# Softmax division moved behind the value product, cross attention by pairs of tiles, last residuals on ScalarE and GpSimd

## The chip, the core and the metric

The kernel runs on one core of a Trainium2 chip. The core has TensorE (PE; its weight loads are shown apart, as PEld), VectorE (DVE), ScalarE (ACT), GpSimd (POOL) and SyncE (SP, which issues most transfers). Each works through its own instruction queue in order; semaphores order them against each other. The metric is the device time of one execution in microseconds, here the median of three runs.

## What is computed

One decoder block on 2 x 1024 tokens of width 256, all in float32: self attention with 16 heads and a relative bias, cross attention onto 77 context tokens with 16 heads of width 16, and a mixture of 8 experts, two chosen per token. Each part is a residual on a normalised input. Cut to what the change touches:

```python
x = x + self_attention(layernorm(x))       # ends in its own layernorm with gamma_a, beta_a

q, k, v = heads(layernorm(x) @ Wq), heads(ctx @ Wk), heads(ctx @ Wv)   # q, k divided by DK ** 0.25
scores = where(mask == 0, -1e9, q @ k.T)   # (2, 16, 1024, 77)
attn = softmax(scores)                     # over the 77 context tokens
x = x + concat_heads(attn @ v) @ Wu + bu

h = layernorm(x)
x = x + layernorm(0.5 * gelu(h @ shared_W + shared_b)
                  + sum of the two best experts of softmax(h @ gate_W)) * gamma + beta
```

## The kernel before

**Layout.** `xs` holds all tokens in SBUF as 16 tiles of 128 tokens; four tiles are a chunk `c` (0 to 3). All PSUM tiles up to the experts come from one ring of eight banks (`one`, line 83), reused in program order.

**Stages.** A loop over `n` runs the two streams of self attention (`stream_a`, `stream_b`, `times_v`), with small jobs put between them by the tables `between`, `settle` and `ask`. There are 16 halves `h` of attention, four for each chunk; `collect(h)` divides by the sums and writes a chunk's output to a tile `o`, which is normalised and added to `xs`. For chunks 0 and 1 `settle` does this in the streams, with ScalarE and GpSimd. For chunks 2 and 3 (`h` 14 and 15) it is done behind the streams by VectorE, in `o_gamma` (line 1083) and `o_add` (line 1089): eight instructions per chunk.

**Order.** Behind the loop the order is written out by hand as a list of words (line 1124 on). The program issues them one after the other, so the list fixes each engine's own queue. `exps_b` and `times_v` are the end of the streams; at `close` the streams' buffers are given up and SyncE loads weights for the experts' routing; `weights` starts the first expert's load.

**Cross attention**, for each tile `i`: `scores` (TensorE, four banks), `masked` (VectorE adds the mask and takes the row maxima), `less` (GpSimd subtracts them), `exps` (ScalarE), `sums` (VectorE sums 77 columns per head and takes the reciprocal), `shares` (GpSimd multiplies all 16 x 77 exponentials by it), `turn` (TensorE transposes 16 heads, ScalarE copies them into `PT`). For each chunk: `attend(c, G)` (the values times `PT`, 512 columns, copied to `oT` by ScalarE) and `output(c, u)` (times `Wu`, added to `xs` by VectorE). `query` and `q_*` prepare a chunk's queries; `add_bu` adds the bias.

**Routing.** When a chunk has its output, `stats`, `dev`, `off`, `norm` normalise it and store it to `xnd`, `flip` transposes it, `gate` computes the logits, `choose`, `rank`, `place`, `hots` and `invert` find the expert slots of its tokens, and after the last chunk `owners` and `pick` give the rows that the experts gather. `shared` (the shared layer) is put between. Chunks 0 and 1 form one group of routing, chunks 2 and 3 one each. The experts' loop follows; its gathers go to `xgs`.

**Normalisation.** `norm_scale` (line 134) adds the epsilon on VectorE and raises to the power -0.5 on GpSimd. `offsets` (line 167) makes the offset on VectorE, and `scale` (line 178) applies both on ScalarE.

## Time and profile before

| what | value |
|---|---|
| three runs | 976.96, 978.7 and 988.31 us, median 978.7 |
| profiled execution | 986.99 us; span from first to last instruction 985.3 us |
| mean granted TensorE clock | 0.965 of full |
| PE busy | 922.7 us (94% of the span) |
| DVE busy | 579.4 us (59%) |
| ACT busy | 544.1 us (55%) |
| POOL busy | 403.5 us (41%) |
| last `times_v` ends | about 501.8 us |
| `pick` starts | 666.9 us |

The profile is one execution, and its times are microseconds from its first instruction. Line numbers (L700) are those of the kernel before. In a row of groups, `out<-in` names the tiles, `x12` the count, then come the busy time of all and the mean ns of one, then the engine's idle time just ahead of them and what ended it. A granted clock of 1.00 is full speed. TensorE's matmuls in float32 are recorded twice each, transposes once.

### The profile page before, as it was taken

The numbers are of one execution on the slowest core, as the hardware profiler recorded it, in microseconds if no ns is written. First come the engines' busy times: TensorE is split into PE (matmuls) and PEld (weight loads), VectorE is DVE, ScalarE is ACT, GpSimd is POOL, SyncE is SP. The second block draws the span as 40 slices with busy tenths as digits, with TensorE's granted clock in tenths as the row PEclk, the third lists the DMA queues.
The fourth block names the chain that finished last, engine by engine and source line by source line (L and its number), as shares of the span: only waits on it lengthen the run. The fifth ranks groups of instructions, "written<-read, shape, count | busy, mean of one in ns | idle before, by whom it ended". The sixth has DMA issues, their size and how long they took to land.

```text
span 985.3 us, 16174 instructions
## 1 busy us (share of the span) xinstructions
PE 922.7 (94%) x6080; PEld 542.9 (55%) x6080; DVE 579.4 (59%) x1172; ACT 544.1 (55%) x1079; POOL 403.5 (41%) x344
## 2 busy tenths in 40 slices
PE   9999999999999999999947999998999999999983
...
DVE  5874668878888797987589998471111031011117
...
PEclk9999999999999999999976999689999999999997
...
GB/s 172 59 1 2 2 2 1 2 1 1 2 1 2 1 2 1 1 1 1 1 0 18 1 23 22 27 17 264 307 196 156 206 180 153 206 308 329 132 145 125
DMA packets 65162, 75.62 MB, mean 77 GB/s; under 512 B 17967, under 2 KB 57036, under 8 KB 65076
## 3 DMA queue, kind: packets, MB, share of 16 engines
...
## 4 chain that ended last, share of the span: by engine, by line
PE 72%; DVE 15%; DMA 9%; issue 2%; ACT 1%; POOL 1%; SPq 0%; DVEq 0%; POOLq 0%; ACTq 0%
PE sA L549 14%; PE av L612 13%; PE sB L595 11%; PE po L1515 9%; PE ph L1496 9%; DMA pairs<-y,to_row 7%; PE pp L502 3%; PE pb L394 2%; PE pv L340 1%; DVE cm L700 1%; DVE cs L712 1%; PE pq L664 1%; DVE scrap L696 1%; PE idle L252 1%; DVE xs L1094 1%
## 5 line engine op out<-in xcount | busy, mean ns | idle before, releaser
L556 DVE TENSOR_REDUCE mx<-sA 128x1 f32<-128x512 f32 x512 | 317.4, 683 | 95.4 <-PE sB L595 88.4
L603 ACT ACTIVATE pt<-sB 128x512 f32<-128x512 f32 x512 | 264.8, 603 | 63.1 <-PE sB L595 63.0
L549 PE MATMUL sA<-kT,scrap 32*128 32x512 f32 x1024 | 253.8, 619 | 0.0
L595 PE MATMUL sB<-qB,kT 32*128 32x512 f32 x1024 | 247.6, 616 | 0.0
L625 POOL TENSOR_TENSOR avs<-avs,part 128x512 f32<-128x512 f32 x112 | 142.1, 1269 | 231.0 <-ACT part L624 225.7
L1503 ACT ACTIVATE hT<-ph,b1s 128x256 f32<-128x256 f32 (+1 forms) x184 | 77.7, 424 | 184.6 <-PE ph L1496 179.7
L549 PEld LDWEIGHTS sA<-kT,scrap 32*128 32x128 f32 x1024 | 100.4, 183 | 82.3 <-ACT pt L603 54.5
L612 PE MATMUL av<-pt,vaug 128*32 128x512 f32 x1024 | 137.4, 605 | 3.2 <-DVE mx L556 3.2
L595 PEld LDWEIGHTS sB<-qB,kT 32*128 32x128 f32 x1024 | 97.7, 183 | 37.9 <-issue 30.1
L1522 DVE TENSOR_TENSOR y<-po,b 128x512 f32<-128x512 f32 (+1 forms) x23 | 13.0, 564 | 176.4 <-PE po L1515 169.7
L1496 PE MATMUL ph<-xgT,w 128*128 128x256 f32 (+1 forms) x576 | 109.3, 334 | 1.3 <-DMA w<-in_L_ffn_W_dram 0.7
L1515 PE MATMUL po<-w,hT 128*128 128x256 f32 x432 | 105.2, 382 | 3.4 <-DVE y L1522 3.3
L1496 PEld LDWEIGHTS ph<-xgT,w 128*128 128x128 f32 x576 | 91.3, 191 | 21.4 <-ACT hT L1503 7.5
L1515 PEld LDWEIGHTS po<-w,hT 128*128 128x128 f32 x432 | 77.7, 190 | 14.4 <-DVE y L1522 5.5
L1526 POOL DMA_INDIRECT pairs<-y,to_row x35 | 35.3, 1007 | 115.1 <-DMA pairs<-y,to_row 79.4
L1466 POOL DMA_INDIRECT xg<-xnd,from_row x35 | 34.3, 979 | 104.5 <-PE px L1482 64.2
L612 PEld LDWEIGHTS av<-pt,vaug 128*32 128x32 f32 x1024 | 21.0, 109 | 100.4 <-DVE mx L556 91.4
L624 ACT COPY part<-av 128x512 f32<-128x512 f32 x108 | 65.7, 609 | 5.4 <-PE av L612 5.1
L138 POOL TENSOR_TENSOR rstd<-rstd,nhalf 128x4 f32<-128x4 f32 x20 | 21.7, 1084 | 71.2 <-DVE rstd L137 70.8
L729 ACT COPY PT<-ppT 77x512 f32<-77x512 f32 x64 | 32.7, 588 | 2.2 <-PE ppT L728 1.5
L1515 PE MATMUL po<-xnT,hT 128*128 128x256 f32 x128 | 31.8, 383 | 1.9 <-DVE y L1522 1.9
L194 PE MATMUL pxT<-ident,xn 128*128 128x128 f32 x96 | 17.5, 305 | 16.7 <-ACT xn L184 16.6
...
## 6 DMA issues: line engine op xcount, KB each, us to landing
...
```

What stands on the lines that cost most here:

```text
L549: nc.tensor.matmul(s, lhsT=units[h // 4, "q"][r0 : r0 + 32, q0 : q0 + P], rhs=units[h // 4, "k", g % 2][r0 : r0 + 32, 512 * kh : 512 * kh ...
L556: nc.vector.tensor_reduce(largest[h][:, qt, hh : hh + 1, kh], s, AX.X, ALU.max)
L595: nc.tensor.matmul(s, lhsT=units[h // 4, "k", g % 2][r0 : r0 + 32, kt * P : (kt + 1) * P], rhs=shifted[h][r0 : r0 + 32, :], start=True, st ...
L603: nc.scalar.activation(powers[m, hh], s, AF.Exp, scale=1.0 / 16.0)
L612: nc.tensor.matmul(av[32 * hh : 32 * hh + 32, :], lhsT=vaug[:, kt, 4 * g + hh, :, b], rhs=powers.pop((m, hh)), start=True, stop=True,)
L624: copy(part, av)
L625: nc.gpsimd.tensor_tensor(sums[h], sums[h], part, ALU.add)
L1466: fetched[i] = nc.gpsimd.indirect_dma_start(out=xg[:, s, :], out_offset=None, in_=xnd[:, :], in_offset=bass.IndirectOffsetOnAxis(ap=from_r ...
L1496: nc.tensor.matmul(ph[:, hc % group, :], lhsT=w1[:, kc, hc * P : (hc + 1) * P], rhs=xgT[:, kc, :], start=(kc == 0), stop=(kc == 1),)
L1503: hidden[i] = nc.scalar.activation(hT[:, hc, :], ph[:, hc % group, :], AF.Gelu, bias=b1s[:, i, hc : hc + 1])
L1515: nc.tensor.matmul(po[:, s, :], lhsT=hT[:, hc, s * P : (s + 1) * P], rhs=w2[:, hc, :], start=(hc == 0), stop=(hc == NH - 1),)
L1526: nc.gpsimd.indirect_dma_start(out=pairs[:, :], out_offset=bass.IndirectOffsetOnAxis(ap=to_row[:, k : k + 1], axis=0), in_=y[:, s, :], in_ ...
```

## The change

The exponentials are transposed as they are. A new `fold` on GpSimd adds columns 38 to 75 of a head to columns 0 to 37 and copies column 76, so VectorE sums 39 columns instead of 77; ScalarE spreads the 16 reciprocals over 256 columns (`wide`). `shares` is gone. A new `divisors(k)` transposes the spread reciprocals of two tiles and copies them to `oT`; `attend(k)`, now for a pair of tiles, multiplies them by the product with the values on VectorE. `output(k)` is also by pairs. For chunks 2 and 3 of self attention the residual is done as in `settle`: `o_off` and `o_norm` with ScalarE, `o_gamma` and `o_add` by halves on GpSimd. The epsilon and the offsets move to GpSimd everywhere. The `o` tiles move to a pool that stays open, and the experts' gather buffers `xgs` are laid into them. There are 27 idle matmuls at the start instead of 30, and the list of words is a new one.

```diff
@@ -122,6 +122,7 @@
     xnT = const.tile([P, 2, N], F32, name="xnT")
+    kept = ctx.enter_context(tc.tile_pool(name="kept", bufs=1))
     keep = ExitStack()
@@ -134,7 +135,7 @@
         r = small.tile([P, 4], F32, tag="rstd", name="rstd")
-        nc.vector.tensor_scalar(r[:, :n], mv[:, :, 1], eps, None, ALU.add)
+        nc.gpsimd.tensor_scalar(r[:, :n], mv[:, :, 1], eps, None, ALU.add)
         nc.gpsimd.tensor_tensor(r[:, :n], r[:, :n], nhalf[:, :n], ALU.pow)
@@ -168,9 +169,10 @@
         if live is not None:
-            nc.vector.tensor_tensor(r[:, :4], r[:, :4], live, ALU.mult)
+            nc.gpsimd.tensor_tensor(r[:, :4], r[:, :4], live, ALU.mult)
         off = small.tile([P, 4], F32, tag="off", name=f"off{c}")
-        nc.vector.scalar_tensor_tensor(off, mv[:, :, 0], -1.0, r[:, :4], ALU.mult, ALU.mult)
+        nc.gpsimd.tensor_tensor(off, mv[:, :, 0], r[:, :4], ALU.mult)
+        nc.gpsimd.tensor_scalar(off, off, -1.0, None, ALU.mult)
         if dst is None:
@@ -248,7 +250,7 @@
     idle = one("idle")
-    for _ in range(30):
+    for _ in range(27):
         nc.tensor.matmul(idle[:, :P], lhsT=ident, rhs=ident, start=True, stop=True)
@@ -627,7 +629,7 @@
         if (b, qb) not in outs:
-            outs[b, qb] = kp.tile([P, 4, D], F32, tag="o", name=f"o{b}{qb}", bufs=2)
+            outs[b, qb] = kept.tile([P, 4, D], F32, tag="o", name=f"o{b}{qb}", bufs=2)
         o, avs = outs[b, qb], sums.pop(h)
@@ -687,7 +689,7 @@
-    maxima = {}
+    maxima, halved, one_over = {}, {}, {}
@@ -707,57 +709,78 @@
+    def fold(i):
+        st, half = sts[i % 4], T2 // 2
+        halved[i] = cr2.tile([P, H, half + 1], F32, tag="halved", name=f"halved{i}")
+        nc.gpsimd.tensor_tensor(
+            halved[i][:, :, :half], st[:, :, :half], st[:, :, half : 2 * half], ALU.add
+        )
+        nc.gpsimd.tensor_copy(halved[i][:, :, half:], st[:, :, 2 * half :])
     def sums_of(i):
-        maxima[i] = small.tile([P, H], F32, tag="cs", name="cs")
-        nc.vector.tensor_reduce(maxima[i], sts[i % 4], AX.X, ALU.add)
-        nc.vector.reciprocal(maxima[i], maxima[i])
-    def shares(i):
-        st, cs = sts[i % 4], maxima.pop(i)
-        nc.gpsimd.tensor_tensor(st, st, cs.unsqueeze(2).to_broadcast([P, H, T2]), ALU.mult)
+        cs = small.tile([P, H], F32, tag="cs", name="cs")
+        rc = small.tile([P, H], F32, tag="rc", name="rc")
+        nc.vector.tensor_reduce(cs, halved.pop(i), AX.X, ALU.add)
+        nc.vector.reciprocal(rc, cs)
+        one_over[i] = cr2.tile([P, H, DH], F32, tag="wide", name=f"wide{i}", bufs=4)
+        nc.scalar.copy(one_over[i], rc.unsqueeze(2).to_broadcast([P, H, DH]))
     def turn(i):
-        c, t = i // 4, i % 4
-        if c not in PTs:
-            PTs[c] = cr2.tile([P, H, 512], F32, tag="PT", name=f"PT{c}")
+        k, t = i // 2, i % 2
+        if k not in PTs:
+            PTs[k] = cr2.tile([P, H, 2 * P], F32, tag="PT", name=f"PT{k}")
         st = sts[i % 4]
-        for k in range(4):
+        for q in range(4):
             pp = one("ppT").rearrange("p (h f) -> p h f", f=P)
             for h in range(4):
-                nc.tensor.transpose(pp[:T2, h, :], st[:, 4 * k + h, :], ident)
-            nc.scalar.copy(PTs[c][:T2, 4 * k : 4 * k + 4, P * t : P * t + P], pp[:T2, :, :])
-    def attend(c, G):
-        b, PT = c // 2, PTs[c]
-        if c not in oTs:
-            oTs[c] = cr2.tile([P, 2, 512], F32, tag="oT", name=f"oT{c}")
-        po = one("pco")
-        for i in range(2):
-            for r in range(4):
-                h = 8 * G + 2 * r + i
-                nc.tensor.matmul(
-                    po[32 * r : 32 * r + 32, :],
-                    lhsT=vx[:T2, b, h, :, :].rearrange("p i d -> p (i d)"),
-                    rhs=PT[:T2, h, :],
-                    start=(i == 0),
-                    stop=(i == 1),
+                nc.tensor.transpose(pp[:T2, h, :], st[:, 4 * q + h, :], ident)
+            nc.scalar.copy(PTs[k][:T2, 4 * q : 4 * q + 4, P * t : P * t + P], pp[:T2, :, :])
+    def divisors(k):
+        oTs[k] = cr2.tile([P, 2, 2 * P], F32, tag="oT", name=f"oT{k}")
+        pr = one("pr").rearrange("p (g f) -> p g f", g=2)
+        for t in range(2):
+            rc = one_over.pop(2 * k + t).rearrange("p h d -> p (h d)")
+            for G in range(2):
+                nc.tensor.transpose(
+                    pr[:, G, P * t : P * t + P], rc[:, P * G : P * G + P], ident
                 )
-        nc.scalar.copy(oTs[c][:, G, :], po)
-    def output(c, u):
+        nc.scalar.copy(oTs[k], pr)
+    def attend(k):
+        b, PT = k // 4, PTs.pop(k)
+        po = one("pco").rearrange("p (g f) -> p g f", g=2)
+        for G in range(2):
+            for i in range(2):
+                for r in range(4):
+                    h = 8 * G + 2 * r + i
+                    nc.tensor.matmul(
+                        po[32 * r : 32 * r + 32, G, :],
+                        lhsT=vx[:T2, b, h, :, :].rearrange("p i d -> p (i d)"),
+                        rhs=PT[:T2, h, :],
+                        start=(i == 0),
+                        stop=(i == 1),
+                    )
+        nc.vector.tensor_tensor(oTs[k], oTs[k], po, ALU.mult)
+    def output(k):
         pu = one("pu").rearrange("p (t f) -> p t f", f=D)
+        oT = oTs.pop(k)
         for t in range(2):
 ...
                     pu[:, t, :],
-                    lhsT=oTs[c][:, G, P * (2 * u + t) : P * (2 * u + t) + P],
+                    lhsT=oT[:, G, P * t : P * t + P],
                     rhs=cwu[:, G, :],
 ...
                 )
-        x2 = xs[:, 4 * c + 2 * u : 4 * c + 2 * u + 2, :]
+        x2 = xs[:, 2 * k : 2 * k + 2, :]
         nc.vector.tensor_tensor(x2, x2, pu, ALU.add)
@@ -1078,20 +1101,23 @@
-    def o_gamma(h):
+    def o_off(h):
         c, o = out_of(h)
-        mv = moments.pop(("o", c))[1]
-        for t in range(4):
-            nc.vector.scalar_tensor_tensor(
-                o[:, t, :], o[:, t, :], mv[:, t, 0:1], gamma_a, ALU.subtract, ALU.mult
-            )
-    def o_add(h):
+        offsets(("o", c), None, o)
+    def o_norm(h):
         c, o = out_of(h)
-        r = tokens.pop(("o", c))
-        for t in range(4):
-            x1 = xs[:, 4 * c + t, :]
-            nc.vector.scalar_tensor_tensor(x1, o[:, t, :], r[:, t : t + 1], x1, ALU.mult, ALU.add)
+        scale(("o", c), range(4), o)
+    def o_gamma(h, u):
+        o2 = out_of(h)[1][:, 2 * u : 2 * u + 2, :]
+        g2 = gamma_a.unsqueeze(1).to_broadcast([P, 2, D])
+        nc.gpsimd.tensor_tensor(o2, o2, g2, ALU.mult)
+    def o_add(h, u):
+        c, o = out_of(h)
+        x2 = xs[:, 4 * c + 2 * u : 4 * c + 2 * u + 2, :]
+        nc.gpsimd.tensor_tensor(x2, x2, o[:, 2 * u : 2 * u + 2, :], ALU.add)
@@ -1105,6 +1131,8 @@
         o_dev=o_dev,
+        o_off=o_off,
+        o_norm=o_norm,
         o_gamma=o_gamma,
@@ -1112,7 +1140,8 @@
         sums=sums_of,
-        shares=shares,
+        fold=fold,
+        divisors=divisors,
         q_stats=measure,
@@ -1123,36 +1152,38 @@
         exps_b:119 times_v:118:1 exps_b:120 times_v:119:1 exps_b:121 times_v:120:1
-        exps_b:122 times_v:121:1 collect:14 exps_b:123 times_v:122:1 o_stats:14
-        exps_b:124 times_v:123:0 scores:0 o_dev:14 exps_b:125 masked:0 times_v:124:0
-        exps_b:126 times_v:125:0 exps_b:127 times_v:126:0 o_gamma:14 scores:1 masked:1
-        less:1 scores:2 masked:2 o_add:14 times_v:127:0 less:0 collect:15 exps:1
-        q_stats:2 q_dev:2 o_stats:15 exps:0 o_dev:15 sums:0 o_gamma:15 q_off:2 less:2
-        sums:1 exps:2 o_add:15 sums:2 shares:0 q_norm:2 q_stats:3 close shares:1
-        q_flip:2:1 add_bu:2 shares:2 scores:3 masked:3 q_flip:2:0 turn:0 less:3 scores:4
-        q_dev:3 exps:3 masked:4 turn:1 sums:3 less:4 shares:3 scores:5 exps:4 masked:5
-        turn:2 sums:4 query:2:1 query:2:0 less:5 shares:4 constant:0 scores:6 exps:5
-        masked:6 turn:3 sums:5 less:6 shares:5 constant:1 scores:7 exps:6 attend:0:0
-        masked:7 attend:0:1 turn:4 sums:6 q_off:3 less:7 shares:6 constant:2 scores:8
-        q_norm:3 exps:7 masked:8 output:0:1 stats:0:1 output:0:0 q_flip:3:1 add_bu:3
-        turn:5 sums:7 less:8 shares:7 constant:3 scores:9 q_flip:3:0 exps:8 masked:9
-        turn:6 sums:8 less:9 shares:8 constant:4 scores:10 query:3:0 exps:9 masked:10
-        query:3:1 turn:7 sums:9 less:10 shares:9 constant:5 scores:11 stats:0:0 exps:10
-        attend:1:0 masked:11 dev:0 attend:1:1 turn:8 sums:10 off:0 less:11 norm:0
-        shares:10 constant:6 scores:12 exps:11 masked:12 output:1:1 stats:1:1 output:1:0
-        turn:9 sums:11 less:12 shares:11 constant:7 scores:13 exps:12 masked:13
-        flip:0:1:0 flip:0:0:0 turn:10 sums:12 gate:0 less:13 shares:12 constant:8
-        scores:14 exps:13 masked:14 turn:11 sums:13 less:14 shares:13 constant:9
-        scores:15 stats:1:0 exps:14 attend:2:0 masked:15 dev:1 attend:2:1 turn:12
-        sums:14 off:1 less:15 norm:1 shares:14 exps:15 output:2:1 output:2:0 turn:13
-        sums:15 shares:15 stats:2:1 flip:1:1:0 stats:2:0 flip:1:0:0 turn:14 dev:2 gate:1
-        choose:0 earlier:1 turn:15 attend:3:0 attend:3:1 off:2 rank:0 place:0 output:3:0
-        stats:3:0 output:3:1 norm:2 stats:3:1 dev:3 flip:2:1:0 flip:2:0:0 shared:0:0
-        hots:0:0 off:3 hots:1:0 norm:3 gate:2 hots:0:1 flip:3:1:1 choose:1 flip:3:0:0
-        shared:1:1 gate:3 shared:3:0 rank:1 earlier:2 invert:0 choose:2 place:1 hots:2:0
-        rank:2 hots:2:1 totals shared:3:1 hots:1:1 invert:1 place:2 hots:3:0 shared:0:1
-        hots:3:1 filled:0 invert:3 owners invert:2 shared:2:0 filled:1 weights filled:2
-        filled:3 pick shared:2:1 rows biases shared:1:0
+        exps_b:122 times_v:121:1 collect:14 exps_b:123 times_v:122:1 exps_b:124
+        times_v:123:0 scores:0 masked:0 exps_b:125 times_v:124:1 exps_b:126
+        times_v:125:0 o_stats:14 exps_b:127 times_v:126:1 scores:1 o_dev:14
+        times_v:127:0 masked:1 scores:2 less:1 collect:15 o_off:14 exps:1 o_stats:15
+        less:0 o_norm:14 o_dev:15 o_gamma:14:0 exps:0 o_off:15 close o_add:14:0
+        o_gamma:14:1 o_add:14:1 o_norm:15 masked:2 q_stats:2 fold:0 o_gamma:15:1
+        o_gamma:15:0 fold:1 less:2 q_dev:2 q_off:2 sums:0 turn:0 o_add:15:0 turn:1
+        sums:1 o_add:15:1 scores:3 masked:3 exps:2 fold:2 divisors:0 attend:0 turn:2
+        less:3 q_stats:3 q_norm:2 scores:4 exps:3 q_flip:2:1 add_bu:2 masked:4 sums:2
+        q_flip:2:0 output:0 stats:0:0 turn:3 fold:3 sums:3 less:4 query:2:0 scores:5
+        exps:4 q_dev:3 masked:5 divisors:1 attend:1 turn:4 fold:4 sums:4 less:5 q_off:3
+        scores:6 exps:5 q_norm:3 masked:6 output:1 stats:0:1 turn:5 fold:5 sums:5 less:6
+        dev:0 scores:7 exps:6 query:2:1 masked:7 off:0 divisors:2 norm:0 attend:2 turn:6
+        fold:6 sums:6 less:7 scores:8 exps:7 q_flip:3:1 add_bu:3 q_flip:3:0 constant:0
+        masked:8 output:2 stats:1:0 turn:7 fold:7 sums:7 constant:1 less:8 flip:0:1:1
+        flip:0:0:1 scores:9 exps:8 constant:2 masked:9 divisors:3 gate:0 constant:3
+        attend:3 turn:8 fold:8 sums:8 less:9 constant:4 scores:10 exps:9 query:3:1
+        constant:5 masked:10 output:3 stats:1:1 turn:9 fold:9 sums:9 constant:6 less:10
+        query:3:0 dev:1 scores:11 exps:10 constant:7 masked:11 off:1 divisors:4
+        constant:8 norm:1 attend:4 turn:10 fold:10 sums:10 less:11 constant:9 scores:12
+        exps:11 masked:12 output:4 stats:2:0 turn:11 fold:11 sums:11 less:12 flip:1:1:1
+        flip:1:0:0 scores:13 exps:12 masked:13 divisors:5 gate:1 choose:0 attend:5
+        turn:12 fold:12 sums:12 less:13 scores:14 exps:13 rank:0 masked:14 output:5
+        stats:2:1 turn:13 fold:13 sums:13 place:0 less:14 dev:2 hots:1:1 off:2 scores:15
+        exps:14 divisors:6 norm:2 masked:15 attend:6 turn:14 flip:2:1:0 hots:0:1 fold:14
+        flip:2:0:0 sums:14 earlier:1 less:15 output:6 gate:2 exps:15 shared:1:0 turn:15
+        choose:1 hots:0:0 rank:1 fold:15 sums:15 divisors:7 place:1 stats:3:0 attend:7
+        earlier:2 output:7 stats:3:1 invert:0 shared:2:1 dev:3 hots:2:1 off:3 norm:3
+        shared:0:1 filled:0 flip:3:1:0 flip:3:0:0 hots:2:0 hots:1:0 gate:3 invert:1
+        choose:2 invert:2 rank:2 filled:1 shared:2:0 filled:2 totals shared:1:1
+        shared:0:0 place:2 hots:3:1 hots:3:0 invert:3 owners filled:3 pick weights rows
+        shared:3:0 biases shared:3:1
     """.split()
@@ -1448,7 +1479,7 @@
         ff2 = later.enter_context(tc.tile_pool(name="ff2", bufs=1))
-        xgs = [ff2.tile([P, 2, D], F32, name=f"xg_{k}") for k in range(3)]
+        xgs = [outs[1, k // 2][:, 2 * (k % 2) : 2 * (k % 2) + 2, :] for k in range(3)]
         xgTs = [ff2.tile([P, 2, 2 * P], F32, name=f"xgT_{k}") for k in range(2)]
```

## The prediction

> **What bounds the kernel now.** I read the page's slices first, to find where TensorE is not busy at full clock: only slices 20 to 27, some 490 to 690 us.
>
> ```profile
> PE   9999999999999999999947999998999999999983
> DVE  5874668878888797987589998471111031011117
> PEclk9999999999999999999976999689999999999997
> ```
>
> Before it the two attention streams hold TensorE, after it the experts do; the change leaves both nearly alone. So I asked for the busy time of each engine in stretches of 10 us (PE, PEld, DVE, ACT, POOL, granted clock, DMA share, GB/s):
>
> ```profile
> 500.00:510.00 10.00, 2.68 (x16) 0.95 (x14) 9.86 (x15) 3.05 (x3) 7.43 (x5) 0.79 0.00 0
> 510.00:520.00 10.00, 0.00 (x0) 0.00 (x0) 9.66 (x21) 1.23 (x1) 7.07 (x5) 0.50 0.00 0
> ...
> 550.00:560.00 10.00, 10.00 (x70) 6.32 (x62) 9.86 (x15) 5.69 (x10) 8.72 (x8) 1.00 0.00 0
> ...
> 590.00:600.00 10.00, 10.00 (x87) 6.82 (x89) 9.79 (x19) 5.91 (x11) 9.44 (x7) 1.00 0.00 0
> ...
> 620.00:630.00 10.00, 10.00 (x42) 6.41 (x33) 1.41 (x7) 3.14 (x6) 0.00 (x0) 0.50 0.16 54
> ```
>
> Three stages: an opening (500 to 540), VectorE full and TensorE empty or at half clock; a middle (540 to 612), both full; a tail (612 to 667, where `pick` starts), TensorE busy but at half clock from 614 to 632. The chain of work that ended last gives the opening to VectorE's residuals and the tail to TensorE:
>
> ```profile
> 505.00 4.01 DVE xs L1094 x4
> ...
> 515.92 5.14 DVE o L1085 x4
> ...
> 522.97 5.59 DVE xs L1094 x4
> ...
> 616.44 6.98 PE pco L739 x32
> ...
> 626.94 6.21 PE pu L753 x16
> ```
>
> In the middle the chain names VectorE, but the windows show TensorE equally full: freeing VectorE there gives nothing. The prices, from the groups by shape, 480 to 690 us:
>
> ```profile
> L718 POOL TENSOR_TENSOR scrap<-scrap,cs 128x1232 f32<-128x1232 f32 x12 | 27.3, 2272 | 5.4 <-DVE cs L713 5.4
> L705 POOL TENSOR_TENSOR scrap<-scrap,cm 128x1232 f32<-128x1232 f32 x12 | 27.2, 2266 | 3.1 <-DVE cm L700 2.5 <-PE pu L753 0.6
> L712 DVE TENSOR_REDUCE cs<-scrap 128x16 f32<-128x1232 f32 x12 | 17.1, 1427 | 0.0
> L1085 DVE SCALAR_TENSOR_TENSOR o<-o,bnmv('o', 3)_5809,gamma_a 128x256 f32<-128x256 f32 x4 | 5.2, 1364 | 0.0
> L1085 DVE SCALAR_TENSOR_TENSOR o<-o,bnmv('o', 2)_5617,gamma_a 128x256 f32<-128x256 f32 x4 | 2.7, 747 | 0.0
> ```
>
> **Streams, before 490 us.** `offsets` goes from one VectorE instruction (0.15 us) to two or three on GpSimd, and the epsilon add too. GpSimd's tiny casts cost 0.19 us, so 0.4 to 0.6 us a call; it is 59% idle. Only the queue matters: at chunks 0 and 1, `scale` on ScalarE follows `offsets` at once, and the GpSimd queue then holds an accumulation (308.20 to 309.47) ahead of it. ScalarE's scale, at 308.04 now, waits till about 310, with the next exponentials behind it: 0 if they catch up, 2 us each if not; I take 1 us, twice, +2. Three idle matmuls fewer: 60 records took 9.86 us, six are 0.7 to 1.0 us, and the first transposes (11.1 us) stand right behind them with their first tile ready at about 9.4: -0.7. Sum +1.3 (0 to +4).
>
> **Opening.** The 16 VectorE instructions of L1085 and L1094 (2.7+5.2+9.8=17.7 us) go; ScalarE gets 8 of 0.59 (`o_norm`), GpSimd 8 of 1.28 (the 128x512 rows of L991), 10.2 us. Here the Trainium skill speaks against the change: GPSIMD Engine Reference, "3.1 Elementwise — side-by-side cycle accounting", has a two-input add on GpSimd cost 1.96 times VectorE's, as a reason to keep elementwise work on VectorE. By that, GpSimd's 10.2 us would be 5.2 us on VectorE and the move a loss. The rows have VectorE at 1.36 us for 256 columns while GpSimd streams (0.75 otherwise), GpSimd at 1.28 for 512: here VectorE pays more. I go by the rows; but GpSimd becomes the opening's bound. Its queue from the last accumulation (about 502.7): five `less` 11.0; halves of gamma and residual 10.0; four `fold`; two `dev` 2.4; offsets 1.25; bias add 0.7; `add_bu` 2.35.
>
> `fold` is in no row. Its near rows are GpSimd's two-operand adds: 256 columns 0.73, 512 1.27, 1024 2.36, so 608 columns 1.48, and 0.2 for the copy: 1.7. Bounds: 1.2 (`less`'s 1.83 ns per column) and 3.4 (strided 38-of-77 rows at double). Four are 6.8. Sum 34.5; from 502.7, with 3 us of waits (`add_bu` for ScalarE's `q_norm`, `fold:2` for its exponentials), `less:4` ends at about 540 and its exponentials at 541.5; `turn:4` starts at about 542.5. Now it starts at 552.9: -10.4. TensorE idles meanwhile and starts cold, as now. New wait: ScalarE's `wide` copy of tile 0 waits for `fold:0` (516.7) and VectorE, and the copies of `turn:0` and `turn:1` stand behind it, then TensorE's `divisors:0` at 523. GpSimd hides this wait until 540.
>
> **Middle.** VectorE gets lighter: the sum over 39 instead of 77 columns is 0.8 for 1.43; a pair's multiply is 0.6 to 0.7 (as L761), and the 1.2 to 2.2 us that a four-column offset costs it beside GpSimd go. GpSimd has fold 1.7 for shares 2.25. The loop exps (1.23), fold, less (2.25), two hops is 5.3 us a tile. ScalarE's `wide` copy must be in before the next exps: 1.7+0.8+0.25+hops after the exps, 0.9 us earlier than less. TensorE is the bound, at warm durations from starts of successive groups: turn 1.88, scores 1.24, a query half 1.77, a flip pair 0.93, gate 1.78, shared 1.73; two attends of 512 columns 3.57, so a pair's is 1.79; two outputs 3.55, so 1.78. `divisors` is four transposes of L728's kind, 0.47 (cold 0.9). From `turn:4` to `turn:15` the new list has 11 turns 20.7, 10 scores 12.4, 6 outputs 10.7, 5 attends 8.9, 5 divisors 2.4, 3 query halves 5.3, 4 flip pairs 3.7, 3 gates 5.3, rank 1.7, shared 1.7: 73 us. Now the stretch is 61.0 (552.9 to 613.9), with fewer attends, outputs, gates in it: +12. In the new list each `turn` stands directly behind its exps; by my walk they are ready 0.5 to 2.6 us ahead. I add 2.5 for misses.
>
> **Tail.** Now 53.0 us (613.9 to 666.9). `attend:3` and `output:3` cover four tiles at half clock, 6.98+6.21 us; half of each goes into the middle. Also into it: `rank:0` (3.4, cold), its choose and place, gate 2, two `hots` (1.7 each on VectorE). What stays is a chain: turn 1.9, divisors and copy 1.1, attend 1.8, multiply 0.7, output 1.8, residual and statistics 1.8, dev and off 1.8, norm 2.1, flips and copy 1.6, gate 1.8, choose 2.6, rank and place 2.6, hots 3.4, invert 1.9, owners 4.7, pick 0.5: 32, and 2 for part of it cold: 34, -19. On the clock, TensorE: Matmul & The Clock Gate, "What's actually happening", says one idle window of 3.4 us halves it. The rows differ: the drop at 614 followed 1.26 us of idling at 610.8 and then gates of 8 columns. By the page the new tail, filled by `shared`, stays warm (32 us); by the row its gates can cost it 4 to 8 us.
>
> **At no cost.** `xgs` in the `o` tiles: last read near 528, gathers at 669; 140 us hide it. A smaller PT keeps two buffers, each read within two pairs; the stores of xnd only move with `norm`.
>
> **Sum.** +1.3-10.4+12+2.5-19 = -13.6: the profiled execution, 986.99 us (span 985.3 and 1.7 around it), would take 973. The runs' median is 8.3 us below it; the same difference applies, 978.7-13.6 = 965. What is late next is TensorE's own work.
>
> **The rivals.**
> - *The tail stays warm, the middle has no misses, GpSimd's opening overlaps* (chance 0.35): 2+2.5+3+1.3 us better, 956. For it: TensorE was 97 to 100% busy in the middle. Against it: shorter lead of exps over turn.
> - *The gain stays off the path* (0.18): opening bound by GpSimd at fold 2.5 (+3), tail cold (+7), and each tile 0.3 us late (+3): 978. For it: VectorE's chain in the middle was never alone.
> - *TensorE goes cold in the middle* (0.13), slower than before. Place: `turn` behind `fold`. If fold takes 3.4 us, the loop is 7.0+hops, 7.3, against TensorE's 6.6 a tile: beyond 3 us of fold TensorE starts to wait in each tile. Middle +7, opening +7; and if half of the 73 us then runs at half clock, +23: 1002. Against it: no GpSimd add in the trace costs twice its neighbour.
>
> My forecast has 0.34. Below 949 and above 988 lie under 0.2 together, mostly the cold case. A difference of 2%, 19.6 us, is about what this kernel's measurement tells from none (its runs spread from 976.96 to 988.31): below 959 lie most of the first rival and the forecast's edge, 0.40; above 998 0.13.
>
> **What would show it.** Right: TensorE's first `ppT` near 510, `turn:4` near 542; fold's add near 1.5 us; the middle with TensorE full; `pick` near 654. Wrong: TensorE idle behind exps in the middle, a clock of 0.5 there, ScalarE waiting for VectorE's `rc`, or streams longer by over 4 us.

## The result, and the profile after

The changed kernel takes 987.77 us (median of 20 executions, 986.01 to 995.73), the kernel before beside it 981.12 us (20 executions, 976.96 to 989.8). The ratio is 1.0064, 95% interval 1.0039 to 1.0089: slower by 6.6 us, clear of the noise of these runs though under 1%, where 965 was forecast. The profiled execution takes 986.09 us, span 984.4.

In all comparisons of this study the kernel before was timed 228 times: 170 executions lie below 985 us, 167 of them at 977 to 983, and 58 above, 55 of them at 987 to 991. The profile that the prediction was made against, 986.99 us, belongs to the upper group; the changed kernel's 20 are all above 985. What parts the two groups is shown with the first experiments.

The page's slices of the changed kernel (busy tenths in 40 slices, then the granted clock):

```profile
PE   9999999999999999999968999788999999999883
DVE  5775658878887797887466879770111031001117
PEclk9999999999999999999977999899999999999997
```

Counted from 0, slices 20 and 21 (492 to 541 us) have TensorE at 6 and 8 tenths for 4 and 7, and VectorE at 6 and 6 for 8 and 9. Slices 25 and 26 (615 to 664 us) are new: TensorE at 7 and 8 where it had 9, with VectorE at 7 and 7 for 4 and 7. Busy time by stretches of 10 us, changed kernel (PE, PEld, DVE, ACT, POOL, granted clock, DMA share, GB/s):

```profile
500.00:510.00 10.00, 2.67 (x21) 1.20 (x14) 6.63 (x18) 5.05 (x7) 9.75 (x12) 0.75 0.15 43
510.00:520.00 10.00, 7.30 (x35) 7.07 (x37) 4.40 (x11) 4.10 (x9) 9.83 (x11) 0.67 0.01 2
550.00:560.00 10.00, 10.00 (x86) 6.48 (x84) 8.05 (x18) 9.40 (x19) 9.61 (x9) 1.00 0.17 55
590.00:600.00 10.00, 9.95 (x96) 7.88 (x96) 9.73 (x18) 4.68 (x9) 7.11 (x6) 1.00 0.00 0
610.00:620.00 10.00, 7.32 (x70) 5.40 (x68) 9.76 (x20) 6.85 (x13) 5.66 (x7) 1.00 0.15 52
620.00:630.00 10.00, 7.16 (x53) 6.13 (x51) 9.45 (x32) 4.41 (x8) 1.42 (x2) 1.00 0.01 2
```

GpSimd, not VectorE, is full in the opening, as forecast. In the middle VectorE is lighter up to 590 (8.05 for 9.86 from 550 to 560), then over 9.4 until 630, and from 600 on fuller than TensorE, which falls to 7.2. The chain that ended last, changed kernel, shows what VectorE does there (start, us, what):

```profile
598.25 2.10 DVE cand L832
...
612.40 2.00 DVE row L911 x4
...
618.01 2.35 DVE col L904
...
624.10 1.26 DVE hots L839
...
630.53 2.85 PE pco L761 x32
...
634.21 3.80 PE pu L776 x8
...
648.51 5.28 PE pin L922 x32
```

The first four belong to the routing's own words, `choose` and `hots`, among the last masks and sums; the last three are TensorE wholly or in part at half clock. The groups by shape, changed kernel, 480 to 690 us, that answer to those of before:

```profile
L707 POOL TENSOR_TENSOR scrap<-scrap,cm 128x1232 f32<-128x1232 f32 x12 | 27.0, 2248 | 2.5 <-DVE cm L702 1.2 <-DVE logits L809 1.1
...
L716 POOL TENSOR_TENSOR halved<-scrap 128x608 f32<-128x608 f32 x12 | 15.6, 1303 | 15.8 <-ACT scrap L710 15.6
...
L725 DVE TENSOR_REDUCE cs<-halved 128x16 f32<-128x624 f32 x16 | 12.6, 786 | 2.9 <-POOL halved L719 2.9
...
L1115 POOL TENSOR_TENSOR o<-o,gamma_a 128x512 f32<-128x512 f32 x4 | 5.0, 1263 | 0.0
```

The prices of the prediction hold: fold 1.30 and 0.21 for its copy (1.7 was taken for both), the sum 0.79 (0.8), the residual's halves 1.26 (1.28).

Where the stages begin and end, in us of each profile (`residual_only` and `before_warm` are experiments that keep the order of before, and stand for its usual execution, of which no profile exists; the forecast's marks include its 1.3 us for the streams):

| | `turn:4` | `turn:15` | `pick` | span | middle | tail | behind `pick` |
|---|---|---|---|---|---|---|---|
| before, as profiled | 552.90 | 613.90 | 666.91 | 985.3 | 61.0 | 53.0 | 318.4 |
| residual_only | 551.54 | 613.54 | 660.23 | 978.8 | 62.0 | 46.7 | 318.6 |
| before_warm | 552.68 | 613.68 | 658.51 | 980.2 | 61.0 | 44.8 | 321.7 |
| forecast for after | 543.8 | 619.3 | 653.3 | | 75.5 | 34 | |
| after | 544.01 | 624.01 | 664.50 | 984.4 | 80.0 | 40.5 | 319.9 |

### The profile page after: what moved, and what is told of

The parts are those of the page before. It is cut to its first block, busy times and chain, and to the rows that moved or that the text cites. A ratio compares the mean times of both kernels' runs of the same rounds, so it can differ in the third digit from the quotient of the medians.

```text
span 984.4 us, 16549 instructions
## 1 busy us (share of the span) xinstructions
PE 927.2 (94%) x6234; PEld 549.3 (56%) x6234; DVE 553.5 (56%) x1131; ACT 550.3 (56%) x1099; POOL 412.3 (42%) x422
## 4 chain that ended last, share of the span: by engine, by line
PE 72%; DMA 10%; DVE 9%; POOL 3%; SPq 2%; issue 1%; ACT 1%; DVEq 0%; POOLq 0%
PE sA L551 14%; PE av L614 13%; PE sB L597 11%; PE po L1546 9%; PE ph L1527 9%; DMA pairs<-y,to_row 7%; PE pp L504 2%; PE ppT L738 2%; PE pb L396 2%; PE pq L666 1%; PE pco L761 1%; PE sC L683 1%; PE pu L776 1%; DVE y L1553 1%; PE pm L577 1%
## 5 line engine op out<-in xcount | busy, mean ns | idle before, releaser
L1497 POOL DMA_INDIRECT o<-xnd,from_row x35 | 34.1, 973 | 96.5 <-PE px L1513 66.5
L738 PE MATMUL ppT<-ident,scrap 128*77 128x128 f32 x192 | 29.2, 316 | 6.5 <-ACT scrap L710 6.2
L1527 PE MATMUL ph<-xgT,xnT 128*128 128x256 f32 (+1 forms) x160 | 31.5, 341 | 1.6 <-ACT hT L1534 1.6
```

Of the source, the lines that this page charges most:

```text
L738: nc.tensor.transpose(pp[:T2, h, :], st[:, 4 * q + h, :], ident)
L1527: nc.tensor.matmul(ph[:, hc % group, :], lhsT=w1[:, kc, hc * P : (hc + 1) * P], rhs=xgT[:, kc, :], start=(kc == 0), stop=(kc == 1),)
```

## The experiments

### Which execution was predicted against

**before_again**: the kernel before, unchanged.

> The kernel before, unchanged, profiled anew. Theory A (the profile misled me): the profiled execution of before (987 us) lost about 9 us to a half clock of TensorE between 614 and 632 us that most executions, near 980 us, do not have; then this profile, if it is one of 980 us, shows the same opening and middle (turn:4 near 553, turn:15 near 614), full clock behind 614 and pick near 658, and the granted clock goes with the time from run to run. Theory B (the loss is in the new order alone): a profile of 980 us has the half clock in the tail too, and what is shorter lies elsewhere, in the streams or the experts.

Measured: 980.09 us (22 executions, 977.4 to 987.99). Its profile is again of the upper group, 987.99 us, with half clock from about 612 to 632 and 54.2 us from `turn:15` to `pick`. The granted clock was also recorded for every execution of before, outside the first 20: the 52 upper ones have a mean of 0.960 to 0.966, the 156 others of 0.965 to 0.975, as theory A said. The 0.008 between the averages of the groups is, by an estimate, some 15 us at half clock, which cost half of that.

**residual_only**: the kernel before with the residuals of chunks 2 and 3 as in the changed one, all else in the order of before.

```diff
-    def o_gamma(h):            # four instructions on VectorE
+    def o_off(h): ...          # offsets
+    def o_norm(h): ...         # ScalarE
+    def o_gamma(h, u): ...     # GpSimd, by halves
-    def o_add(h):              # four instructions on VectorE
+    def o_add(h, u): ...       # GpSimd, by halves
```

> The kernel before with one part of the change: the residuals of chunks 2 and 3 by ScalarE and GpSimd, the rest and the order of tiles as before. Theory G (the opening is bound by VectorE's residuals): turn:4 starts some 8 to 10 us earlier than at 553 and pick moves with it, time 970 to 974. Theory H (GpSimd takes over as the bound of the opening, or VectorE and TensorE, both full in the middle, take the gain back): 978 to 983.

Measured: 980.92 us (20 executions, 977.02 to 988.95), ratio 1.0007, interval 0.9982 to 1.0032. Taking 17.7 us of residual work from VectorE moves `turn:4` by 1.4 us and the time by nothing. So the changed kernel's earlier `turn:4` (544.01) is not owed to the residuals alone. Its list of words has a part in it: `turn:0` no longer stands behind chunk 2's queries, for which TensorE waited 17.5 us here. The new list without the new residuals was not run. Its profile (980.47 us) is of the lower group.

**before_warm**: five idle matmuls ahead of `gate:1` in the kernel before, into the 1.26 us in which TensorE idled at 610.8.

```diff
+    def warm(n):
+        spare_bank = one("warm")
+        for _ in range(n):
+            nc.tensor.matmul(spare_bank[:, :P], lhsT=ident, rhs=ident, start=True, stop=True)
-        turn:14 dev:2 gate:1
+        turn:14 dev:2 warm:5 gate:1
```

> The kernel before with five idle matmuls (128 columns, about 0.6 us at full clock) put ahead of gate:1, into the 1.26 us in which TensorE idled at 610.8. Theory A (the kernel before has two groups of times, 977 to 983 and 986 to 989 us, because half clock behind that idle lasts 6 us in one and 18 to 20 us in the other): with the idle bridged the clock stays at full from 610 to 632, pick starts about 43 to 46 us behind turn:15, and the upper group is gone: runs of 972 to 980, median near 976. Theory A2 (half clock comes from the small matmuls of the gates, not from the idle, and the two groups from elsewhere): clock 0.5 near 614 stays, both groups stay, and the median is that of before plus 0.6, near 981.

Measured: 979.52 us, 22 executions of 976.7 to 982.59, none in the upper group, of which 13 of the 44 of before beside it were; ratio 0.9975, interval 0.9958 to 0.9993. This is the only version here that is faster than both kernels, by 1.6 us; its median is about that of the lower group (980.0). TensorE's timeline of `residual_only`, a stretch of the tail:

```profile
610.73 2.95 PE L779 MATMUL pg<-fgw,xnT 128*128 128x8 f32 x16 [1.26 <-ACT xnT L197]
613.54 3.67 PE L728 MATMUL ppT<-ident,st 128*77 128x128 f32 x16
617.14 4.18 PE L739 MATMUL pco<-PT,vx 77*32 77x512 f32 x32
...
623.06 3.70 PE L753 MATMUL pu<-cwu,oT 128*128 128x256 f32 x16
```

And of `before_warm`:

```profile
610.45 1.36 PE L1105 MATMUL warm<-ident 128*128 128x128 f32 x10
...
613.68 1.95 PE L728 MATMUL ppT<-ident,st 128*77 128x128 f32 x16
615.56 3.64 PE L739 MATMUL pco<-PT,vx 77*32 77x512 f32 x32
...
620.94 3.70 PE L753 MATMUL pu<-cwu,oT 128*128 128x256 f32 x16
```

In the profile of before the same two groups, `pco` and `pu`, took 6.98 and 6.21 us in its chain. With the gap filled both are at full speed; with the gap open, half clock lasts about 7 us in one execution (`residual_only`) and 17 and 20 us in the two profiles of before. In the one predicted against, the four groups from `turn:15` to `pu` take 8.3 us longer than here. The Trainium skill (TensorE: Matmul & The Clock Gate, "What's actually happening") has the activity window run freely and the cold stretch of one kernel differ between executions; these rows show the second, at a price of 8 us, after a pause shorter than the page's window. Taken with the clocks of all executions, and with the upper group gone here, this is the difference between the groups of times, and it accounts for the 8.3 us between the profiled execution and the median, which the prediction had laid outside the change. Theory A holds: the tail that it took 19 us out of was 53.0 us long in about a quarter of the executions, and 45 to 47 us in the others, as far as `residual_only` and `before_warm` stand for them.

### The middle: whose time is it

**late_routing**: the changed kernel with the words of the routing of chunks 0 and 1 (`choose:0`, `rank:0`, `place:0`, `hots`, `earlier:1`, `choose:1`) moved behind `turn:15`, and the tail's own words set behind them.

```diff
-    divisors:5 gate:1 choose:0 attend:5 ... exps:14 rank:0 masked:14 ... sums:13 place:0 less:14
-    dev:2 hots:1:1 off:2 ... flip:2:1:0 hots:0:1 fold:14 ... turn:15 choose:1 hots:0:0 rank:1 fold:15
+    divisors:5 gate:1 attend:5 ... turn:15 fold:15 sums:15 divisors:7 stats:3:0 attend:7 choose:0
+    output:7 stats:3:1 rank:0 ... choose:1 ... rank:1 place:0 ... hots:0:1 hots:0:0 ... hots:1:1
```

> The changed kernel with only its order changed: the routing of chunks 0 and 1 (choose:0, rank:0, place:0, two hots) is put behind turn:15, into the gaps that VectorE has there, as in the order before. Theory C: the chain from 590 to 629 us is VectorE's, because 9 us of routing lie among its last masks and sums; moved, turn:15 starts near 617 (624 now) and the time falls by 5 to 8 us, to 980 to 983. Theory D (the half clock behind turn:15 and the chain of norm, flip and gate set the end anyway): the 7 us come back behind turn:15 and the time stays within 2 us of 988.

Measured: 983.43 us (7 executions, 981.98 to 989.93), ratio to before 1.0053, interval 1.0018 to 1.0087. Busy times of two stretches, `turn:4` to `turn:15` and `turn:15` to `pick`. The changed kernel:

```profile
544.01:624.01 80.00, 76.14 (x605) 57.56 (x601) 68.63 (x145) 53.16 (x96) 50.17 (x68) 0.98 0.06 21
624.01:664.50 40.49, 34.13 (x218) 28.69 (x218) 27.27 (x108) 9.34 (x18) 4.05 (x6) 0.87 0.04 14
```

`late_routing`:

```profile
543.76:618.15 74.39, 73.68 (x589) 55.68 (x585) 57.22 (x112) 52.87 (x95) 51.23 (x70) 0.98 0.07 22
618.15:660.73 42.58, 33.86 (x236) 29.88 (x234) 33.12 (x141) 9.47 (x18) 1.69 (x4) 0.88 0.04 13
```

Without the routing's 11.4 us of VectorE (68.63 less 57.22) the middle is 5.6 us shorter and TensorE idles 0.7 us in all of it. The forecast's "73" for TensorE, less the `rank:0` in it, was 2.4 us short of the 73.68 here (some 1.5 of it, by an estimate from the clock of 0.98, is half clock), and the routing was what stood in its way. The tail gives 2.1 us back. By the times of whole executions alone the gain is not clear of noise, since the intervals of the two ratios overlap; the stages show it.

**spread_routing**: `late_routing` with four of the words put back into the end of the middle, each behind the VectorE operation that TensorE waits for.

```diff
-    masked:15 attend:6                 ... attend:7 choose:0 output:7 stats:3:1 rank:0
+    masked:15 choose:0 attend:6        ... attend:7 earlier:1 output:7 stats:3:1
-    sums:14 less:15 output:6 gate:2    ... sums:15 divisors:7 stats:3:0 attend:7
+    sums:14 less:15 rank:0 output:6 place:0 gate:2 ... divisors:7 stats:3:0 hots:0:1 attend:7
```

> The late_routing order with four of its words put back ahead of the end, each behind the operation of VectorE that TensorE waits for instead of ahead of it: choose:0 behind masked:15, rank:0 behind sums:14, place:0 behind output:6, hots:0:1 behind sums:15. Theory Q (it is not that VectorE has the routing in the middle, but that the words stand ahead of masks and sums in its queue): turn:15 stays at 618 to 619, turn:15 to pick is 38 to 39.5 instead of 42.6, runs 979 to 981, level with the kernel before or just below. Theory R (any VectorE work put among the last tiles delays them, 3 us of it for 2 to 3 us): turn:15 at 621, pick at 660 to 661, 983 as late_routing.

Measured: 988.15 us (22 executions, 985.23 to 995.94), ratio 1.0077: worse than both theories said. The tail did shrink, to 37.8 us, but the middle went to 82.3. TensorE's timeline of `spread_routing`:

```profile
594.86 3.57 PE L761 MATMUL pco<-PT,vx 77*32 77x256 f32 x32
598.36 3.65 PE L738 MATMUL ppT<-ident,scrap 128*77 128x128 f32 x16
...
616.78 0.41 PE L866 MATMUL prk<-taken,before 128*128 128x64 f32 x2 [2.54 <-DVE taken L844]
...
618.56 3.46 PE L776 MATMUL pu<-cwu,oT 128*128 128x256 f32 x8
```

`rank:0` waits for `choose:0` in TensorE's own queue, with `output:6` behind it, and behind the wait `pu` is at half clock, 3.46 us for 1.97. But the half clock at 595 to 602 (3.3 us) lies ahead of all moved words and is not owed to them; `late_routing` had half clock only from about 570 to 573. Theory Q falls, at least for this placing: the wait, `rank:0` and `pu` alone are some 6 us.

**before_extra**: `before_warm` with eight more idle matmuls ahead of each of `turn:5`, `7`, `9`, `11` and `13`. Each eight took 1.79 us from start to next start, not the 1.0 that the expectation reckoned, 8.95 us in all.

```diff
-    turn:5 ... turn:7 ... turn:9 ... turn:11 ... turn:13
+    warm:8 turn:5 ... warm:8 turn:7 ... warm:8 turn:9 ... warm:8 turn:11 ... warm:8 turn:13
```

> before_warm with eight more idle matmuls of 128 columns ahead of each of turn:5, 7, 9, 11 and 13, five times 1.0 us of TensorE (10 records took 1.4 us in before_warm, so 0.13 us each). It gives the kernel before about as much more TensorE work as the divisors of six pairs. Theory S (TensorE is the bound between turn:4 and turn:15 in the kernel before, as the prediction has it): 61 us become 65 to 66 there, and the runs 983 to 985. Theory T (VectorE, 94% busy there, is the bound, and TensorE has only been stretched over it): 61 to 63 us, runs 979 to 981.

Measured: 986.17 us (20 executions), 6.65 above `before_warm`. The middle is 7.4 us longer. `before_warm`:

```profile
552.68:613.68 61.00, 60.13 (x430) 44.58 (x427) 57.20 (x99) 45.20 (x79) 50.40 (x43) 1.00 0.05 18
```

`before_extra`:

```profile
552.94:621.35 68.41, 68.08 (x511) 53.57 (x507) 58.03 (x99) 45.82 (x79) 50.97 (x43) 1.00 0.05 17
```

So 0.83 us of each added microsecond of TensorE comes through, although VectorE was 94% busy in this stretch of `before_warm` (57.20 of 61.00; TensorE 60.13). Theory S holds: in the kernel before, TensorE is the bound of the middle, and work added to it is paid almost in full.

**no_fold**: the changed kernel without `fold`; VectorE sums the 77 columns itself.

```diff
-        nc.vector.tensor_reduce(cs, halved.pop(i), AX.X, ALU.add)
+        nc.vector.tensor_reduce(cs, sts[i % 4], AX.X, ALU.add)
```

> The changed kernel without fold: VectorE sums all 77 columns from the exponentials (1.43 us with GpSimd beside it, for 0.8) and GpSimd loses 1.48 us a tile. Theory K (from turn:4 to turn:15 VectorE is the bound, and what fold takes off it is what it is for): 10 to 12 tiles times 0.6, so 991 to 995. Theory L (VectorE's operations are stretched while GpSimd streams, so that each us of GpSimd taken away gives VectorE back a part of it, 1.48 us less of GpSimd for 0.6 us more of VectorE, and GpSimd's opening gets 6 us shorter): 981 to 986, and the fold was a loss.

Measured: 989.48 us (5 executions, 987.69 to 991.95), 1.7 above the changed kernel's 987.77, between the theories, and not clear of noise. The middle is 82.9 us with VectorE busy 75.0 in it (68.6 with fold), so in the profiles 6.4 us of VectorE buy 2.9 us of the stage: the fold is no loss, and at most a small gain.

**no_division**: spread reciprocals, `divisors` and the multiply left out.

```diff
-        one_over[i] = cr2.tile([P, H, DH], F32, tag="wide", name=f"wide{i}", bufs=4)
-        nc.scalar.copy(one_over[i], rc.unsqueeze(2).to_broadcast([P, H, DH]))
-        pr = one("pr") ...  # four transposes, copied to oT
-        nc.vector.tensor_tensor(oTs[k], oTs[k], po, ALU.mult)
+        nc.scalar.copy(oTs[k], po)
```

> The changed kernel with the division left out: no spread reciprocals, no divisors, and the product with the values is copied to oT by ScalarE instead of being multiplied by VectorE, so the attention's output is that of undivided exponentials; sums and reciprocals are still computed. It takes away 4 x 0.16 us of TensorE, 0.65 us of VectorE and two waits of TensorE (for wide and for oT) per pair. Theory M (the divided path is a good part of the 80 us from turn:4 to turn:15): six pairs, 0.5 to 0.6 us of TensorE each and the waits, 5 to 7 us, and 2 to 3 in the tail: 977 to 981. Theory N (VectorE's routing is the chain there and the division lies beside it): 983 to 987.

Measured: 1007.05 us, which says nothing on the question: with other values in the output the tokens fell differently on the experts (200 passes of the first expert layer's activation in the profile, 184 in the others), and the experts took longer. Up to `pick` the profile can be read: `turn:15` at 617.85, `pick` at 658.75, 6.2 and 5.8 us earlier than in the changed kernel; 5.8 us off the changed kernel's time would be 982, between the theories. Of the 6.2 us, 4.0 are there at `turn:4` (540.00) already, the middle gives 2.2 (77.9, with the clock at 0.93), the tail nothing.

### GpSimd and the opening

**small_on_dve**: the changed kernel with the epsilon and the offsets back on VectorE.

```diff
-        nc.gpsimd.tensor_tensor(off, mv[:, :, 0], r[:, :4], ALU.mult)
-        nc.gpsimd.tensor_scalar(off, off, -1.0, None, ALU.mult)
+        nc.vector.scalar_tensor_tensor(off, mv[:, :, 0], -1.0, r[:, :4], ALU.mult, ALU.mult)
```

> The changed kernel with the epsilon and the offsets back on VectorE. Theory E (they cost through GpSimd's queue, in the streams and in the opening, where GpSimd is full): 3 to 5 us faster. Theory F (they lie in GpSimd's gaps, while VectorE would pay 1 to 2 us for each beside GpSimd's long instructions): within 2 us, or slower by up to 3.

Measured: 991.95 us (4 executions, 989.99 to 992.35), ratio to before 1.0125: 4.2 us above the changed kernel. The profile has `turn:4` at 549.27, 5.3 us later, and the rest as before. Moving these tiny operations to GpSimd is a gain within this change, and all of it lies in the opening.

**no_less**: the changed kernel without the subtraction of the row maxima.

```diff
-    ... masked:15 ... less:15 ... exps:15
+    ... masked:15 ... exps:15
```

> The changed kernel without less: the row maxima are still computed, but GpSimd does not subtract them, and the exponentials are those of the scores as they are (the shares are the same). It takes 2.25 us of GpSimd and one hop out of each tile, and nothing else. Theory O (VectorE's operations with two inputs in SBUF are slowed by GpSimd's long streams: cand 2.09 us for 0.2, col 2.35 for 0.68, row 2.0 for 1.1): without the streams these fall to their short values, 6 to 8 us of VectorE between turn:4 and turn:15, which becomes 72 to 75 us long instead of 80; the opening, which GpSimd bounds, gets 8 to 11 us shorter: 965 to 974. Theory P (the long ones are long for another reason, such as a wait that the record counts as busy): cand, col and row keep their lengths, the middle stays at 78 to 80, and only the opening gains: 975 to 981.

Measured: 983.96 us (20 executions, 977.23 to 990.28), 3.8 below the changed kernel. GpSimd's time from `turn:4` to `turn:15` falls from 50.2 to 26.4 us, and neither stage answers: `turn:4` at 542.89 (544.01), the middle 79.8 (80.0). Where the 3.8 us lie its profile does not show; at 984.44 us it is only 1.7 below that of the changed kernel. Groups of VectorE from `turn:4` to `turn:15`. The changed kernel:

```profile
L911 DVE TENSOR_SCALAR row<-iota_p,part,pair_no 128x128 f32<-128x128 f32 x8 | 3.2, 457 | 0.0
L904 DVE TENSOR_TENSOR col<-part,iota_p 128x512 f32<-128x512 f32 x2 | 3.1, 1562 | 0.0
...
L832 DVE TENSOR_TENSOR cand<-logits,tops 128x64 f32<-128x64 f32 x2 | 2.3, 1158 | 0.1
```

`no_less`:

```profile
L911 DVE TENSOR_SCALAR row<-iota_p,part,pair_no 128x128 f32<-128x128 f32 x8 | 3.2, 460 | 0.0
...
L904 DVE TENSOR_TENSOR col<-part,iota_p 128x512 f32<-128x512 f32 x2 | 1.4, 690 | 0.0
...
L832 DVE TENSOR_TENSOR cand<-logits,tops 128x64 f32<-128x64 f32 x2 | 0.4, 224 | 0.1
```

Theory O is right on the mechanism and wrong on the size: 2.7 us of VectorE came free (68.63 to 65.95), not 6 to 8, and the middle did not get shorter by it. That `row` stayed long does not speak against it. Each of the four long ones of the changed kernel (`cand` at 598.25, `row` at 612.33, `col` at 617.93, `hots` at 624.10) starts inside a GpSimd operation and ends only behind it; for `row` and `hots` that is `fold`, which `no_less` keeps. The changed kernel:

```profile
624.03 1.26 POOL L716 TENSOR_TENSOR halved<-st 128x608 f32<-128x608 f32 x1 [4.22 <-ACT st L710]
...
624.10 1.25 DVE L839 TENSOR_TENSOR hots<-cand,best 128x32 f32<-128x32 f32 x1
```

In `late_routing` none of these operations is lengthened, so 4.6 us of the 11.4 that it took out of the middle were such waiting and not work. In the profile of `no_less` TensorE had half clock from 594 to 601, where `pco` and a turn took 3.53 and 3.68 us for 1.95 and 1.91, so part of a gain may be hidden there.

Three kernels took the opening apart, all from `late_routing`. **open_order** puts `sums:0` behind `turn:1`, so that ScalarE's spread copy of tile 0 no longer stands ahead of its copies of the transposes; **open_warm** puts 24 idle matmuls ahead of `turn:0`; **open_both** does both.

```diff
-    q_off:2 sums:0 turn:0 o_add:15:0 turn:1 sums:1
+    q_off:2 turn:0 o_add:15:0 turn:1 sums:0 sums:1                # open_order
+    q_off:2 sums:0 warm:24 turn:0 o_add:15:0 turn:1 sums:1        # open_warm
+    q_off:2 warm:24 turn:0 o_add:15:0 turn:1 sums:0 sums:1        # open_both
```

> The late_routing order with sums:0 put behind turn:1, so that ScalarE's spread copy of tile 0, which waits for fold:0 at 516.5, no longer stands ahead of its eight copies of turn:0 and turn:1. Theory U (that wait is on the path of the opening: TensorE's scores:3 waits until 518.9 for a bank that these copies free): scores:3 starts at 515 to 516.5, turn:4 3 us earlier, near 541, and the runs come to 980 to 981. Theory V (GpSimd's queue of residuals, fold and less holds turn:2 and turn:3 anyway): scores:3 is earlier but turn:2 stays near 528 and turn:4 near 543.5, runs 983.

Measured: 984.62 us (20 executions, 978.99 to 988.15); `scores:3` at 516.6, `turn:4` at 542.34, 1.4 us earlier than in `late_routing`.

> The late_routing order with 24 idle matmuls ahead of turn:0, in the 6.2 us in which TensorE waits there (0.22 us each at full clock, 5.3 us). It tries the clock of the opening alone: in late_routing TensorE is at half clock from 506 to 530, which by the warm durations of the same groups is 8 to 9 us of its work there. Theory W (TensorE's half clock sets the opening): turn:0 and turn:1 take 3.8 us for 6.3, turn:4 3 to 6 us earlier, runs 978 to 981. Theory V (GpSimd's queue holds it): turn:4 at 543 to 544 and 983; if the idle matmuls themselves run at half clock, turn:0 is 3 us later and turn:4 1 to 3 us later, 984 to 986.

Measured: 988.53 us (20 executions, 982.64 to 992.67); the idle matmuls ran at full clock, the two turns took 3.72 us for 6.13, and `turn:4` stayed at 543.88. The whole is slower than either theory said.

> The late_routing order with both edits of the opening, the 24 idle matmuls and sums:0 behind turn:1. Theory X (each alone leaves the other's wait in place, and both together shorten the opening): turn:4 at 538 to 540, runs 976 to 979, which would be below the kernel before. Theory V (GpSimd's queue): turn:4 near 543, runs 983.

Measured: 987.23 us (22 executions, 981.98 to 991.99); `turn:4` at 541.98. TensorE's timeline of `open_both`:

```profile
510.07 3.72 PE L738 MATMUL ppT<-ident,scrap 128*77 128x128 f32 x32 [0.84 <-ACT scrap L710]
514.43 2.22 PE L683 MATMUL sC<-kbd,scrap 64*128 64x308 f32 x8 [0.64 <-ACT PT L739]
518.61 0.64 PE L748 MATMUL pr<-ident,wide 128*128 128x128 f32 x2 [1.96 <-ACT wide L728]
522.43 0.69 PE L748 MATMUL pr<-ident,wide 128*128 128x128 f32 x2 [3.18 <-ACT wide L728]
523.05 3.64 PE L761 MATMUL pco<-PT,vx 77*32 77x256 f32 x32
```

Turn and scores are 4 us ahead, and then `divisors:0` waits for the spread reciprocals, whose `fold:1` stands behind the residuals on GpSimd. The last of these transposes start near 523 in every version (523.5 in the changed kernel, 523.0 in `no_less`, 522.4 here). Behind them TensorE has work almost without a pause up to `turn:4`. Theory V is the nearer: `turn:4` comes 1.8 us earlier than in `late_routing`, not 4 to 6, so GpSimd's residuals and folds set the opening, and `less`, the order on ScalarE and TensorE's clock are worth little beside them. In `no_less` GpSimd waits 1.9 us for chunk 3's moments, till 508.1, and from there to 520 its queue is the same. What was not tried is the place of the folds in it: in the changed kernel the exponentials of tiles 0 and 1 were ready at 509.9, while `fold:0` ran at 515.4 and `fold:1` at 519.2, behind the residuals.

The two versions with idle matmuls have the longer medians, although at `turn:4` they are at most 1.5 us behind `late_routing` and `open_order`. Why stays open. `open_both` has `pick` at 660.68, as `late_routing` has, and ends 6 us later: its clock is 0.60 and 0.71 from 660 to 680, where it is 0.83 and 1.00 in `late_routing`. The idle matmuls are not shown to be the cause: `open_order`, which has none of them, looks the same behind its `pick` at 661.10, and `open_warm`, with 24, has 1.00 in both stretches. `open_order`:

```profile
660.00:670.00 10.00, 8.90 (x32) 7.54 (x33) 1.95 (x11) 0.59 (x1) 5.97 (x6) 0.63 0.56 175
670.00:680.00 10.00, 8.42 (x29) 6.08 (x29) 1.38 (x2) 3.33 (x6) 5.29 (x5) 0.69 0.98 336
```

### The tail

**late_warm**: `late_routing` with idle matmuls in the three waits of its tail.

```diff
-    attend:7 choose:0 output:7 ... norm:3 rank:1 place:0 ... flip:3:0:0 invert:0
+    attend:7 warm:6 choose:0 output:7 ... norm:3 warm:6 rank:1 place:0 ... flip:3:0:0 warm:20 invert:0
```

> The late_routing order with idle matmuls in the three places where its TensorE waits in the tail: 6 ahead of output:7, 6 ahead of rank:1, 20 ahead of invert:0. In late_routing the clock was 0.83 from 620 to 630 and 0.70 from 630 to 640, which is some 4 to 5 us of half-clock work. Theory I (the part of late_routing's gain that the tail gave back went into the clock): turn:15 to pick 38 to 39 us instead of 42.6, runs 978 to 981, at or just below before. Theory J (the tail is VectorE's chain of choose, place and hots, and TensorE's clock lies beside it): the clock near 1.0 but pick not earlier, 983 to 984 as in late_routing.

Measured: 985.34 us (22 executions, 982.06 to 991.33), ratio 1.0028. Its tail:

```profile
618.58:660.65 42.07, 37.72 (x299) 34.34 (x297) 33.12 (x141) 9.38 (x18) 1.69 (x4) 1.00 0.04 14
```

The clock is 1.00 in all of it, for 0.88 in `late_routing`, and the tail is 0.5 us shorter. TensorE has 30 us of work of its own in these 42 (37.7 less 7.7 of idle matmuls); VectorE has 33 us, in a chain. Theory J holds: once routing stands in the tail, it is VectorE's.

## Why the prediction was wrong

Against the profiled execution of before the forecast was -13.6, and -0.9 came: 12.7 us of error in the working. Another 10 came from the step from profile to median. In the order of its steps:

- **Streams**, +1.3: `scores:0` starts at 490.23, 0.12 later than before. The wait that it named came as named: ScalarE's scale, at 308.04 before, runs at 310.27, having waited 2.23 us for GpSimd's offset. But the streams caught it up; 1.2 too careful. So small a term could not be checked on one profile each: `scores:0` lies at 490.11 and at 488.59 in the two of before.
- **Opening**, -10.4: -9.0, the first `ppT` at 509.91 for "near 510". GpSimd's residuals and folds bound it, as said, and `less:4` ends at 540.4 for "about 540". What failed is the sentence that GpSimd hides the new wait for the spread copy until 540: that wait is the path, and ends at 523. Behind it TensorE's own work, up to about 532 at half clock, leads to 544. That the mark was nearly hit is in part luck.
- **The residual's move**, weighed against the 1.96 of the Trainium skill (GPSIMD Engine Reference, "3.1 Elementwise — side-by-side cycle accounting"): GpSimd takes 1.26 us for 512 columns with two inputs and VectorE 0.68 for its own residual of that size (`xs<-xs,pu`, one input in PSUM), a ratio of 1.85, near the page's. What the ratio does not hold is the waiting of VectorE beside GpSimd, for which the prediction rightly went by the rows. But the move alone was worth nothing (`residual_only`).
- **Middle**, 73 + 2.5: 80.0, 4.5 short. TensorE's sum was nearly right (76.1 busy, with half clock in it). The step that failed is "VectorE gets lighter". The prediction moved `rank:0`, `choose`, `place` and two `hots` out of the tail, entered TensorE's share into the middle (rank 1.7), and VectorE's nowhere. It is 11.4 us, 4.6 of it waiting beside GpSimd, and it stands ahead of masks, sums and multiplies that TensorE waits for; `late_routing` took 5.6 us back by moving it.
- **Tail**, 34: 40.5. By its chain's own terms: `divisors` come 4.1 us late, since `sums:15` stands behind `choose:1` and `hots:0:0` on VectorE; attend and output cost 3.1 more, at half clock; `dev` and `off` 1.1; `rank` and `place` 2.2, since two `invert` at half clock stand ahead of `rank:2`; choose 0.3. That is +10.8. `invert` runs beside `owners` (-1.9), and the 2 for a cold clock is in these numbers: +6.9 by the terms, +6.5 by the marks. ScalarE's wait ahead of this, changed kernel:

```profile
629.63 0.40 ACT L728 COPY wide<-rc 128x256 f32<-128x256 f32 x1 [2.90 <-DVE at L877]
630.56 0.59 ACT L751 COPY oT<-pr 128x512 f32<-128x512 f32 x1 [0.53 <-PE pr L748]
```

- **The clock in the tail.** By the page that the prediction weighed (TensorE: Matmul & The Clock Gate, "What's actually happening"), half clock comes after one idle window of about 3.4 us, so that a tail filled by `shared` would stay warm. It did not: after waits of 1.0 and 1.6 us at 626 and 628.5 the clock was 0.50 from about 631.5 to 638, and again from 649 to 651, behind a gate. The row of before, a drop after 1.26 us, was the better guide, and 4.4 us is what it cost (`pco` 2.9 for 1.9, `pu` 3.8 for 2.0, two `invert` 5.3 for 3.7).
- **At no cost**: the time behind `pick` is 319.9 us, 1.3 to 1.5 longer than in the profiles of before and `residual_only` and 1.8 shorter than in that of `before_warm`, so within what executions differ by there. Whether `xgs` in the `o` tiles has a part in it was not tried.
- **Sum**: -1.2 + 1.4 + 4.5 + 6.5 + 1.5 = 12.7, the error of the working, the last term being what lies behind `pick`.
- **"The same difference applies"**: this step failed by the whole 8.3 us. The difference was no overhead outside the change. It was half clock inside the tail, in one of the slower quarter of executions, and the -19 of the tail had already counted it as gained: against a usual tail of 45 to 47 us, 34 is only 11 to 13 less.

Against `residual_only`, whose profile is of the lower group and whose median is that of before, the account is: opening -7.5, middle +18.0, tail -6.2, behind `pick` +1.3, together +5.6; measured +6.6 between medians.

Why it could hardly pay is in `before_warm` and `before_extra`. From `turn:4` to `pick` `before_warm` takes 105.8 us with TensorE busy for 101.9 of them, so freeing VectorE could win at most 3.9 us there. The change adds the transposes of the reciprocals there (4.3 us of records), and by its order one query half and two tiles' scores fall behind `turn:4` (4.6 us, for 1.9 of an output gone ahead), which takes back most of the 7.5 us of the opening. The rest of the loss is TensorE waiting for VectorE (2.6 us for `oT`, 1.8 for `taken`), for `wide` (2.2), and half clock.

Of the rivals, the first read TensorE as 97 to 100% busy in the middle, which overlooks 560 to 570 with 92%. TensorE cold in the middle for want of `fold` had the wrong place: fold took 1.5 us, and the middle's clock was 0.98; its outcome, slower than before, came by another way. The gain that stays off the path was the nearest with 978, but of its three reasons only the cold tail was seen.
